# A graph and expert network of two layers: four late weight fills at slot 0, five result buffers, and the last sums on both sides of a branch

## The chip, the cores and the metric

The kernel runs on one core of a Trainium2 chip. The time is that of one execution on the device, in microseconds (us); of several runs the median is given. A profile of one more execution lies beside the times. Engines are called as in its rows: PE (TensorE; PEld is its weight load), DVE (VectorE), ACT (ScalarE), POOL (GpSimd), SP (SyncE); a "q" behind the name (SPq, ACTq) is the engine's issuing of transfers and its control instructions.

## What is computed

There are 2708 nodes with 256 features in float32 and a random adjacency matrix with some 1.2% of ones. Two layers follow one another; each is an attention over the graph and then a network of 8 experts, of which every node takes its best two. The part that the change touches is the expert network of the second layer:

```python
def moe(x):                       # 2708 x 256, E = 8, hidden 512
    gate = softmax(x @ gate_w + gate_b)
    w, e = top_k(gate, 2)         # two experts for each node
    out = 0
    for k in range(2):
        h = gelu(x @ W1[e[k]] + b1[e[k]])
        out += w[k] * (h @ W2[e[k]] + b2[e[k]])
    return x + out
```

The kernel computes each expert only for the nodes that chose it.

## The kernel before

**Rows and slots.** Each node's row, with its weight and its number, is scattered to a region of DRAM called `disp`, twice, into the region of each of its two experts. The expert network then works on chunks of 128 rows, one chunk in one "slot". Layer 1 always runs 47 slots (`often`, L1145). The first 20 are laid out before all rows are routed; the others are placed once routing is done (`place_grid`). Should an input need more than 47, a branch (`tc.If(used > often)`, L1986) runs the others. With this input it isn't taken.

**One slot.** `slot(s, s1)` (L1903) does this in the order of the program: it starts late weight fills, if any are due; `up` (L1830) makes the scaled bias `bias2` on ACT (L1837), 16 matmuls for the hidden layer (L1844) and four GELUs on ACT (L1852); `turned(s + 1)` transposes the next slot's rows on DVE (L1817); a step of the routing of the tiles still missing follows (`line.step()`, on DVE, POOL and PE); then `down(s - 1)` (L1858) runs eight matmuls of the slot before (L1860), fetches for slots to come, adds bias and weight to the result `y` on DVE (L1866), and POOL scatters `y` to its rows in `xd` (L1872). `xd1` has two rows for each node, one for each of its experts, so nothing is added there.

**What a slot fetches.** `fetch` (inside `slot`) gets weights three slots ahead by an indirect transfer of POOL (L1750), and the rows of a chunk six slots ahead (L1757, five in layer 0): SP reads the chunk's place from a table (L1762), then issues four transfers of a quarter each into a buffer `xg` (L1769) and one for the weights and numbers into `who` (L1775). `xg` is read by the transpose, `who` by the bias, by `y` and, as addresses, by the scatter; so a buffer of `who` comes free only when the scatter has landed. `y` too is held until its scatter has landed.

**Weights of layer 1.** Eight buffers (`ring`), one for each expert at first. Four are filled ahead; four lie in memory that the attention gives back late and are filled from within the slots by `fill(e)` (L1895), on ACT's queue, 1154 KB each.

**What sets the order.** In layer 1's slots PE, ACT and DVE keep the order of the program (a schedule written by hand, L1800), and SP does so in the whole kernel. Transfers issued by SP and ACT report on eight semaphores, taken in turn in one common order (101 to 108 in the trace); an issue waits until the transfer before it on the same semaphore has landed. POOL's transfers have eight of their own (110 to 117).

**The sums.** The result is `kept` (what came out of the attention) plus both rows of `xd1`. It is formed in parts (L2037ff): `whole_` are four parts of 512 nodes, which early slots have written in full; `rest` are the others (256, 256, 128 and 20 nodes). At the end of slot 40 (`s0`, L2089) SP loads the two rows of each part of `whole_` (8 loads of 512 KB, L2058), behind scatters 0 to 38. Three of the parts are added (L2069, L2070) and stored (L2073) after slots 43 to 45. After the last slot, `ending()` loads all but one part of `rest` on ACT's queue, adds and stores the last part of `whole_`, and loads the last part of `rest`, whose buffer that one had. Then comes the branch, and behind it the adds and stores of `rest` (L2130).

Of the kernel before, what the change touches and what calls it, by code (L numbers as in the profile page):

```python
# [9 lines left out]
F32 = mybir.dt.float32  # L10
# [10 lines left out]
P = 128  # L21
N = 2708
D = 256
# [11 lines left out]
GROUP = 4  # L35
# [64 lines left out]
ROWS_AHEAD = 5  # L100
# [6 lines left out]
def adj_ffn_kernel(ctx: ExitStack, tc: tile.TileContext, a: dict, out: bass.AP):  # L107
    nc = tc.nc
# [3 lines left out]
    rows = ctx.enter_context(tc.tile_pool(name="rows", bufs=3))  # L112
# [242 lines left out]
    class Line:  # L355
# [6 lines left out]
        def add(self, steps):  # L362
            self.waiting.append(steps)
# [765 lines left out]
    class Experts:  # L1129
# [293 lines left out]
                tc.declare_no_dep(start.ins, group=self.groups[2], reason="other rows of xd")  # L1423
                tc.add_to_no_dep_group(self.groups[3], start.ins)

        def behind_results(self, start, but=0):
            self.behind(start, self.results[: len(self.results) - but])

        def behind_written(self, start, last=True):
            self.behind(start, self.written)  # L1430
# [326 lines left out]
        def fetch_rows(self, s):  # L1757

            disp, wide = self.disp, D // GROUP
            xg = self.one.tile([P, GROUP, wide], F32, name="xg", bufs=self.rows_ahead + 2)  # L1760
            who = self.one.tile([P, 2], F32, name="who", bufs=self.rows_ahead + 3)
            at = nc.values_load(  # L1762
                self.token_row[0:1, s : s + 1], min_val=0, max_val=IDLE,
                engines=(mybir.EngineType.SP,),
                skip_runtime_bounds_check_because="a chunk begins below its region's end",
            )
            chunk = disp[bass.ds(at, P), :]
            starts = [
                nc.sync.dma_start(  # L1769
                    xg[g * QUARTER : (g + 1) * QUARTER],  # L1770
                    chunk[:, g * wide : (g + 1) * wide].rearrange("(t i) e -> i t e", t=GROUP),
                )
                for g in range(GROUP)
            ]
            starts.append(nc.sync.dma_start(who, chunk[:, D:]))  # L1775
            for i, start in enumerate(starts):
                if s < FULL_AFTER[self.early]:
                    self.other_rows(start, late=False)
                if s in (0, FULL_AFTER[self.early]):
                    self.behind_written(start, last=(i == GROUP))  # L1780
            return xg, who
# [25 lines left out]
        def slots(self, two, ps_mm, ps_acc, line):  # L1807
            hidden, own_norm, xd = self.hidden, self.own_norm, self.xd
            often = self.often
            _, hc, w2, b2, b1, ln, row = self.packed_weights  # L1810
# [19 lines left out]
            def up(w, xe, factor):  # L1830


                bias2 = two.tile([P, D], F32, name="bias2", bufs=2 if own_norm else 4)
                if own_norm:
                    nc.vector.tensor_scalar(bias2, w[:, b2:b1], factor, None, ALU.mult)
                else:
                    nc.scalar.activation(bias2, w[:, b2:b1], AF.Copy, scale=factor)  # L1837
                hT = two.tile([P, hc, P], F32, name="hT")
                for g in range(0, hc, GROUP):
                    ps = ps_mm.tile([P, GROUP, P], F32, name="mm")  # L1840
                    for i in range(GROUP):
                        f = g + i
                        for c in range(DC):
                            nc.tensor.matmul(  # L1844
                                ps[:, i, :],
                                w[:, c * hidden + f * P : c * hidden + (f + 1) * P],
                                xe[:, c, :],
                                start=(c == 0), stop=(c == DC - 1),
                            )
                    for i in range(GROUP):  # L1850
                        f = g + i
                        nc.scalar.activation(  # L1852
                            hT[:, f, :], ps[:, i, :], AF.Gelu, bias=w[:, b1 + f : b1 + f + 1]
                        )
                return hT, bias2

            def down(s, w, who, hT, bias2, then):
                ps = ps_acc.tile([P, D], F32, name="acc")  # L1858
                for f in range(hc):
                    nc.tensor.matmul(  # L1860
                        ps, hT[:, f, :], w[:, w2 + f * D : w2 + (f + 1) * D],
                        start=(f == 0), stop=(f == hc - 1),
                    )
                then()
                y = two.tile([P, D], F32, name="y", bufs=3)
                nc.vector.scalar_tensor_tensor(  # L1866
                    y, ps, who[:, 1:2], bias2, op0=ALU.mult, op1=ALU.add
                )
                at = bass.IndirectOffsetOnAxis(ap=who.bitcast(I32)[:, 0:1], axis=0)
                if not own_norm:  # L1870

                    start = nc.gpsimd.indirect_dma_start(  # L1872
                        xd[:], at, y, None, bounds_check=2 * N - 1, oob_is_err=False
                    )
                    for i in (2, 5):
                        tc.declare_no_dep(
                            start.ins, group=self.groups[i], reason="other rows of xd"
                        )
                    tc.add_to_no_dep_group(self.groups[2], start.ins)
                    self.results.append(start.ins)  # L1880
                    return
                start = nc.gpsimd.indirect_dma_start(  # L1882
                    xd[:], at, y, None, bounds_check=N - 1, oob_is_err=False, compute_op=ALU.add
                )
                if s < FULL_AFTER[self.early]:
                    tc.declare_no_dep(start.ins, group=self.groups[3], reason="other rows of xd")
                    tc.add_to_no_dep_group(self.groups[2], start.ins)
                self.last_start = start
                return start

            n = FULL_AFTER[self.early]
# [8 lines left out]
            fills = [] if own_norm else list(range(RING, E))  # L1900
            placed, placing, behind, xe = False, None, None, None

            def slot(s, s1):  # L1903
                nonlocal placed, placing, behind, xe
                w, (_, who) = self.weights[s], self.rows_[s]
                for _ in range((2, 0, 1, 1)[s] if s < 4 and fills else 0):
                    fill(fills.pop(0))
                after = turned(1) if s == 0 and not own_norm else None
                hT, bias2 = up(w, xe, who[:, 1:2])
# [57 lines left out]
            with tc.issue_after(self.last_start.ins) if own_norm else ExitStack():  # L1967
                i = 0 if own_norm else 1
# [36 lines left out]
    experts1 = Experts(1, 512, packed1, gb_b, False, xd1, disps[1], 14)  # L2005
# [7 lines left out]
    with tc.tile_pool(name="mask", bufs=1) as mp, ExitStack() as first_masks:  # L2013
# [16 lines left out]
        with tc.tile_pool(name="sum", bufs=1, side="right") as pool:  # L2030
            own = [pool.tile([P, GROUP, D], F32, name=f"y{i}") for i in range(GROUP)]
# [7 lines left out]
            whole_ = [x for x in parts_ if x[0] < DONE_EARLY]  # L2039
            rest = [x for x in parts_ if x[0] >= DONE_EARLY + GROUP]  # L2040
            rest = [(DONE_EARLY, 2, P), (DONE_EARLY + 2, 2, P), *rest]
            places = {x[0]: i % GROUP for i, x in enumerate(whole_ + rest)}

            def rows_of(dst, j, t, n, r):
                if n == 1:
# [3 lines left out]
                return rows_[:, t % GROUP : t % GROUP + n]  # L2049

            def results(t, n, r):
                i = places[t]
                return own[i][:r, :n], free[i][:r, :n]

            def load(parts_, queues, early=0):
                for i, (t, n, r) in enumerate(parts_):
                    for j, queue in enumerate(queues):
                        start = queue.dma_start(results(t, n, r)[j], rows_of(xd1, j, t, n, r))  # L2058
                        if early:
                            tc.declare_no_dep(  # L2060
                                start.ins, group=experts1.groups[2], reason="rows written"
                            )
                            tc.add_to_no_dep_group(experts1.groups[5], start.ins)
                        if i == 0:
                            experts1.behind_results(start, but=int(early))

            def add(t, n, r):
                y, y1 = results(t, n, r)
# [3 lines left out]
            def store(t, n, r):  # L2072
                nc.sync.dma_start(rows_of(out, 0, t, n, r), results(t, n, r)[0])  # L2073

            def again():
                load(whole_, (nc.sync, nc.sync))
                for x in whole_:
                    add(*x)
                    store(*x)
                load(rest, (nc.sync, nc.sync))  # L2080

            def ending():
                load(rest[:-1], (nc.scalar, nc.scalar))
                add(*whole_[-1])
                store(*whole_[-1])
                load(rest[-1:], (nc.scalar, nc.scalar))

            experts1.again, experts1.ending = again, ending
            s0 = experts1.sum_behind + 2  # L2089
            experts1.then = {s0: [partial(load, whole_, (nc.sync, nc.sync), 1)]}  # L2090
            for i, x in enumerate(whole_[:-1]):
                experts1.then[s0 + 3 + i] = [partial(add, *x), partial(store, *x)]
            experts1.run(line)
            for x in rest:
                add(*x)
                store(*x)


# [35 lines left out]
```

## Time and profile before

| | |
|---|---|
| runs of the kernel | 1190.30, 1190.56, 1183.24 us, median 1190.3 |
| the profiled execution | 1172.41 us, span of its instructions 1170.7 us |
| mean granted TensorE clock | 0.992 |
| layer 1's slots | from 974 us to 1152 us of the span |
| PE busy in the stretches of the prediction (974 to 1010, to 1045, to 1135) | 31.9 of 36, 32.6 of 35, 89.0 of 90 us |
| from the end of the last matmul to the end of the span | 18.7 us |

The span runs from the first to the last instruction of the core, and all starts in the views are counted from its beginning. A timeline row has start, length, engine, line, operation, what it writes from what it reads, and how many in a row; in brackets stands how long the engine was idle before and what ended the idle time. Rows of SPq and ACTq are the issuing of transfers, and a long one has waited in it. A row of waits has the total, the number and the longest. "mT" as a target of a load is memory of the masks, used again for the second rows of the sums.

### The profile page before, as it was taken

The numbers are of one execution on the slowest core, as the hardware profiler recorded it, in microseconds if no ns is written. First come the engines' busy times: TensorE is split into PE (matmuls) and PEld (weight loads), VectorE is DVE, ScalarE is ACT, GpSimd is POOL, SyncE is SP. The second block draws the span as 40 slices with busy tenths as digits, with TensorE's granted clock in tenths as the row PEclk, the third lists the DMA queues.
The fourth block names the chain that finished last, engine by engine and source line by source line (L and its number), as shares of the span: only waits on it lengthen the run. The fifth ranks groups of instructions, "written<-read, shape, count | busy, mean of one in ns | idle before, by whom it ended". The sixth has DMA issues, their size and how long they took to land. (4 is left out here: it accounts for less than half of the span.)

```text
span 1170.7 us, 20856 instructions
## 1 busy us (share of the span) xinstructions
PE 1122.7 (96%) x6421; PEld 910.6 (78%) x6421; DVE 648.6 (55%) x2406; ACT 415.4 (35%) x1232; POOL 427.7 (37%) x519
## 2 busy tenths in 40 slices
PE   8989999999999999999999999998999998999993
PEld 5665666666666666689999999997899997988993
DVE  5565777786886877653222222222876778632225
ACT  3222222212222222443333333332676664344441
POOL 3001212121222122453344343332663656866552
PEclk9999999999999999999999999999999999999997
DMA  9678676867754668569665945552100617577346
GB/s 220 135 161 212 172 185 159 241 162 183 219 136 141 154 149 313 160 187 279 186 193 130 334 116 162 139 169 59 56 1 29 214 50 212 146 246 240 79 115 248
DMA packets 198661, 195.88 MB, mean 167 GB/s; under 512 B 90939, under 2 KB 181524, under 8 KB 192520
## 3 DMA queue, kind: packets, MB, share of 16 engines
q1 hardware_dynamic: 172780, 117.51, 40.0%
q0 software_dynamic: 24256, 70.81, 19.0%
q10 hardware_dynamic: 1500, 6.08, 1.5%
q8 instruction: 55, 0.90, 0.3%
q14 instruction: 70, 0.57, 0.2%
HBM read 246.19 MB, written 66.15 MB: 267 GB/s over the span
## 5 line engine op out<-in xcount | busy, mean ns | idle before, releaser
L1844 PEld LDWEIGHTS mm<-xe,ring 128*128 128x128 f32 x2192 | 259.3, 193 | 16.9 <-DVE xe L1817 7.8
L1844 PE MATMUL mm<-xe,ring 128*128 128x128 f32 x2192 | 262.2, 277 | 7.7 <-DVE xe L1817 5.1
L1852 ACT ACTIVATE hT<-mm,ring 128x128 f32<-128x128 f32 x548 | 156.6, 369 | 286.4 <-issue 151.0
L1860 PE MATMUL acc<-ring,hT 128*128 128x256 f32 x1096 | 252.2, 380 | 0.0
L1860 PEld LDWEIGHTS acc<-ring,hT 128*128 128x128 f32 x1096 | 201.3, 190 | 24.9 <-ACT hT L1852 1.2
L650 PEld LDWEIGHTS acc<-v,p 128*128 128x128 f32 (+1 forms) x880 | 160.0, 190 | 62.4 <-issue 37.2
L650 PE MATMUL acc<-v,p 128*128 128x257 f32 (+1 forms) x880 | 202.7, 383 | 0.0
L586 PE MATMUL s<-g,xnT 128*128 128x512 f32 x420 | 200.3, 597 | 0.6 <-DVE mT L605 0.6
L1866 DVE SCALAR_TENSOR_TENSOR y<-acc,who,bias 128x256 f32<-128x256 f32 x92 | 44.4, 482 | 260.4 <-PE acc L1860 236.8
L1560 POOL DMA_INDIRECT disp<-row,to x88 | 91.3, 1038 | 257.4 <-DVE x L670 125.4
L598 ACT ACTIVATE p<-s 128x512 f32<-128x512 f32 x105 | 62.7, 597 | 194.6 <-PE s L586 178.4
L288 POOL TENSOR_TENSOR ln_rs<-ln_rs,minus_half 128x2 f32<-128x2 f32 x88 | 68.4, 778 | 172.5 <-DVE ln_rs L284 120.0
L930 PE MATMUL acc<-parts,m 128*128 128x266 f32 x924 | 126.3, 293 | 0.0
L930 PEld LDWEIGHTS acc<-parts,m 128*128 128x128 f32 x924 | 117.1, 185 | 4.1 <-ACT raw L957 0.9
L586 PEld LDWEIGHTS s<-g,xnT 128*128 128x128 f32 x420 | 76.8, 190 | 55.1 <-issue 50.3
L1750 POOL DMA_INDIRECT ring<-L_ffn_packed,weight_row x76 | 79.9, 1051 | 98.1 <-PE acc L1860 65.6
L601 DVE SCALAR_TENSOR_TENSOR p<-p,mT 128x512 f32<-128x512 f32 x100 | 71.0, 710 | 75.1 <-ACT p L598 74.9
L1882 POOL DMA_INDIRECT xd<-y,who x45 | 70.5, 1568 | 105.8 <-DVE xe L1823 53.6
L897 ACT CAST m<-mT 128x512 fp32r<-128x512 fp8e4 (+4 forms) x168 | 71.8, 475 | 9.7 <-PE acc L930 6.3
L1872 POOL DMA_INDIRECT xd<-y,who x47 | 49.6, 1056 | 44.9 <-DVE y L1866 40.0
L272 DVE SCALAR_TENSOR_TENSOR row<-x,wr_rows 128x256 f32<-128x256 f32 x128 | 54.4, 425 | 3.3
L1823 DVE TENSOR_SCALAR xe<-xe_raw,ring 128x128 f32<-128x128 f32 x90 | 27.2, 351 | 39.7 <-DMA ring<-L_ffn_packed,weight_row 38.7
(337 smaller groups left out, 1073.6 us busy)
## 6 DMA issues: line engine op xcount, KB each, us to landing
adj<-in_adj_dram SPq DMA_DIRECT2D x100, 256.0 KB
L_ffn_packed<-in_L_ffn_W_dram SPq DMA_DIRECT2D x32, 512.0 KB
xg<-disp SPq DMA_DIRECT2D x368, 32.0 KB
L_ffn_packed<-in_L_ffn_W_dram SPq DMA_DIRECT2D x32, 256.0 KB
neighbours<-mT SPq DMA_DIRECT2D x5, 1408.0 KB
mT<-neighbours SPq DMA_DIRECT2D x5, 1408.0 KB
ring<-L_ffn_packed SPq DMA_DIRECT2D x3, 2182.0 KB
xin<-in_x_dram SPq DMA_DIRECT2D x42, 128.0 KB
```

The source lines that it names most:

```text
L288: nc.gpsimd.tensor_tensor(rs[:r, 1], rs[:r, 0], minus_half[:r], ALU.pow)
L586: nc.tensor.matmul(ps[:kr, :nb], xnT[:, c, k0 : k0 + kr], g[:, c, :nb], start=(c == 0), stop=(c == DC - 1 and k < KEYS),)
L601: nc.vector.scalar_tensor_tensor(p, p, LARGEST, mask, op0=ALU.min, op1=ALU.mult)
L650: nc.tensor.matmul(accs[j][:r], p[keys, q0 : q0 + r], v[keys, k, :], start=(k == 0), stop=(k == NT - 1),)
L897: nc.scalar.copy(m[:, : q1 - q0], MASKS[b].of_key(mTs[b], k)[:, q0 - b * BN : q1 - b * BN],)
L930: nc.tensor.matmul(acc[:r], masks[t], parts[:, k, i], start=(k == 0 and i == 0), stop=False,)
L1560: nc.gpsimd.indirect_dma_start(disp[:], bass.IndirectOffsetOnAxis(ap=to[:r, j : j + 1], axis=0), rows2[:r, j], None,)
L1750: nc.gpsimd.indirect_dma_start(w, None, packed[:], bass.IndirectOffsetOnAxis(ap=self.weight_row[:, s : s + 1], axis=0), bounds_check=E * P ...
L1844: nc.tensor.matmul(ps[:, i, :], w[:, c * hidden + f * P : c * hidden + (f + 1) * P], xe[:, c, :], start=(c == 0), stop=(c == DC - 1),)
L1852: nc.scalar.activation(hT[:, f, :], ps[:, i, :], AF.Gelu, bias=w[:, b1 + f : b1 + f + 1])
L1860: nc.tensor.matmul(ps, hT[:, f, :], w[:, w2 + f * D : w2 + (f + 1) * D], start=(f == 0), stop=(f == hc - 1),)
L1882: start = nc.gpsimd.indirect_dma_start(xd[:], at, y, None, bounds_check=N - 1, oob_is_err=False, compute_op=ALU.add)
```

## The change

Six things are changed:

1. All four late fills start at slot 0 (before: two at slot 0, one each at slots 2 and 3).
2. `y` has five buffers in layer 1 (before 3), `bias2` three (before 4).
3. `xg` has `ROWS_AHEAD + 2` buffers, that is 7 in both layers (before 8 in layer 1), and `who` three more than before (12 in layer 1, 11 in layer 0).
4. The loads of the early sums are issued at the end of slot 39 (before: 40). The set of scatters that they wait for stays 0 to 38, but the exemption of the loads from scatters (`declare_no_dep`) is gone.
5. `ending()` loads all of `rest` with one row of each pair on SP's queue and the other on ACT's, and adds and stores the last part of `whole_` and all of `rest` ahead of the branch. Behind the branch nothing is left. In the branch, `again()` does all sums anew.
6. For that the parts of `rest` lie in buffers 0 (both halves), 1 and 2, which the parts stored early had.

```diff
-        def behind_results(self, start, but=0):
-            self.behind(start, self.results[: len(self.results) - but])
+        def behind_results(self, start):
+            self.behind(start, self.results)
...
-            xg = self.one.tile([P, GROUP, wide], F32, name="xg", bufs=self.rows_ahead + 2)
-            who = self.one.tile([P, 2], F32, name="who", bufs=self.rows_ahead + 3)
+            xg = self.one.tile([P, GROUP, wide], F32, name="xg", bufs=ROWS_AHEAD + 2)
+            who = self.one.tile([P, 2], F32, name="who", bufs=self.rows_ahead + 6)
...
-                bias2 = two.tile([P, D], F32, name="bias2", bufs=2 if own_norm else 4)
+                bias2 = two.tile([P, D], F32, name="bias2", bufs=2 if own_norm else 3)
...
-                y = two.tile([P, D], F32, name="y", bufs=3)
+                y = two.tile([P, D], F32, name="y", bufs=3 if own_norm else 5)
...
-                for _ in range((2, 0, 1, 1)[s] if s < 4 and fills else 0):
+                while fills:
                     fill(fills.pop(0))
...
-            places = {x[0]: i % GROUP for i, x in enumerate(whole_ + rest)}
+            places = {x[0]: (i, 0) for i, x in enumerate(whole_)}
+            places.update({x[0]: p for x, p in zip(rest, ((0, 0), (0, 2), (1, 0), (2, 0)))})
...
                         if early:
-                            tc.declare_no_dep(
-                                start.ins, group=experts1.groups[2], reason="rows written"
-                            )
                             tc.add_to_no_dep_group(experts1.groups[5], start.ins)
                         if i == 0:
-                            experts1.behind_results(start, but=int(early))
+                            experts1.behind_results(start)
...
                 load(rest, (nc.sync, nc.sync))
+                for x in rest:
+                    add(*x)
+                    store(*x)
 
             def ending():
-                load(rest[:-1], (nc.scalar, nc.scalar))
-                add(*whole_[-1])
-                store(*whole_[-1])
-                load(rest[-1:], (nc.scalar, nc.scalar))
+                load(rest, (nc.sync, nc.scalar))
+                for x in (whole_[-1], *rest):
+                    add(*x)
+                    store(*x)
...
-            experts1.then = {s0: [partial(load, whole_, (nc.sync, nc.sync), 1)]}
+            experts1.then = {s0 - 1: [partial(load, whole_, (nc.sync, nc.sync), 1)]}
...
             experts1.run(line)
-            for x in rest:
-                add(*x)
-                store(*x)
```

More of the change, by code (lines that the diff above doesn't have):

```diff
@@ L2051, in results @@
             def results(t, n, r):
-                i = places[t]
-                return own[i][:r, :n], free[i][:r, :n]
+                i, j = places[t]
+                return own[i][:r, j : j + n], free[i][:r, j : j + n]
             def load(parts_, queues, early=0):
```

## The prediction

> **What bounds the kernel now.** I read the busy table and its slices first, then busy time by stage, the waits of layer 1's expert network, and the timelines around each edit.
>
> ```profile
> PE 1122.7 (96%) x6421; PEld 910.6 (78%) x6421; DVE 648.6 (55%) x2406; ACT 415.4 (35%) x1232; POOL 427.7 (37%) x519
> ```
>
> TensorE is busy 96% of the span, so only its gaps are to be won. By stage (columns: stretch, length, then busy us of PE, PEld, DVE, ACT, POOL, the granted clock, DMA share, GB/s):
>
> ```profile
> 974.00:1010.00 36.00, 31.88 (x215) 28.11 (x215) 25.90 (x130) 14.43 (x44) 27.45 (x31) 1.00 0.71 217
> 1010.00:1045.00 35.00, 32.59 (x223) 30.02 (x222) 16.40 (x64) 13.85 (x45) 26.75 (x28) 1.00 0.66 184
> 1045.00:1135.00 90.00, 89.01 (x607) 83.36 (x607) 22.22 (x52) 39.41 (x127) 51.64 (x51) 1.00 0.54 153
> ```
>
> Those are the 47 slots of layer 1, which start up() every 3.51 us where nothing waits. By the starts of up(), slots 2 to 8 lose 6.0 us (routing on POOL and DVE is their bound), slot 14 loses 2.6, slot 17 0.5, slot 26 1.4: 10.6 in all. After 1152.0 no matmul runs and 18.7 us of ending follow. The change touches three places: slot 0, slots 14 and 17, and slot 40 with the ending.
>
> **The four fills.** Before, two late weight buffers (1154 KB each) are filled at slot 0, the others at slots 2 and 3. The SyncE and ScalarE timelines:
>
> ```profile
> 974.34 5.95 SPq L1769 DMA_DIRECT2D xg<-disp  x4
> 982.02 2.93 SPq L1769 DMA_DIRECT2D xg<-disp  x4
> ```
> ```profile
> 974.13 0.83 ACTq L1896 DMA_DIRECT2D ring<-L_ffn_packed  x2
> 985.20 0.33 ACTq L1896 DMA_DIRECT2D ring<-L_ffn_packed  x1
> 985.63 0.51 ACT L1837 ACTIVATE bias<-ring,who 128x256 f32<-128x256 f32 x1 [3.61 <-DMA xg<-disp]
> 991.44 0.37 ACTq L1896 DMA_DIRECT2D ring<-L_ffn_packed  x1
> 991.86 0.51 ACT L1837 ACTIVATE bias<-ring,who 128x256 f32<-128x256 f32 x1 [4.69 <-DMA xg<-disp]
> ```
>
> The trace's transfers, each with its semaphore and its landing, show the rule here: an issue of SP or ACT first waits until the previous transfer on its semaphore has landed; eight semaphores go round in one order for both queues. So fill 3 waited for a piece of row 3 (landed 985.18) and held ScalarE, as fill 4 did. Before that cost little, because routing was later still. At slot 0 the same waits stand ahead of bias(0), gelu(0) and thus of down(0).
>
> Fills 1 and 2 took semaphores six places apart. If I go on at that spacing, fill 3 takes that of row 3's first piece (landed 980.77, behind fill 1), and fill 4 that of row 4's first piece, which lands behind fill 3. Fills land 4.31 apart (979.95, 984.26), so fill 3 lands at 988.6 and row 4's piece at about 989. ScalarE issues fill 4 then, loads its table (1.28 at 978.14 before), and gelu(0) starts at about 991.2 instead of 979.44; down(0) follows at 991.6 (was 979.86, +11.7), its y at 993.5 (was 984.62, +8.9). VectorE keeps program order, so routing steps and turns behind that y move with it: +8.9. Some 1 us of the later ScalarE holds is given back.
>
> Here a rule speaks against the change. The longest gap inside these slots is 2.24 us and the granted clock stays 1.00, so no row shows TensorE after a long idle. The Trainium skill, "TensorE: Matmul & The Clock Gate", part 1 ("What's actually happening"), says an idle window of about 3.4 us halves the clock until it has been busy as long again. After 11.7 us idle that is an estimated 1.7 us; by the row it is 0. I take the rule: **fills +9.6**.
>
> A second rule speaks for the change: "DMA: Bandwidth & Descriptors", "Queues, rings and completion order", says each DMA engine takes turns between queue rows packet by packet. Then rows of SP would slip between the fills and cost some 0. The trace says otherwise: row 3's second piece, issued 974.84, landed 984.61, just behind fill 2 (984.26), where pieces elsewhere take 1.4 to 1.9. The measurement decides. Bounds: if ScalarE isn't held, row 3 lands behind all four fills at about 993, its turn moves from 986.34 by 7, less 1: +6. Below: 0, if rows slip through; a gain only up to the 6 that these slots lose, which the routing chain excludes. Above: +12, with fill 4 behind one more fill.
>
> **Five y buffers.** y(s) waits until scatter(s-3) has landed; POOL issues these late, behind routing, pads and weights. VectorE's waits and slot 14:
>
> ```profile
> DVE y L1866 <- DMA xd<-y,who: 18.9, 7, 5.4
> ```
> ```profile
> 1031.40 0.48 DVE L1866 SCALAR_TENSOR_TENSOR y<-acc,who,bias 128x256 f32<-128x256 f32 x1 [4.30 <-DMA xd<-y,who]
> 1031.80 0.43 DVE L1817 STREAM_TRANSPOSE xe<-xg 128x256 f32<-128x256 f32 x1
> ...
> 1032.29 1.94 PE L1844 MATMUL mm<-xe,ring 128*128 128x128 f32 x15 [2.24 <-DVE xe L1817]
> ```
>
> y(11) waits 4.30, the turn of slot 14 stands behind it, and TensorE idles 2.24. With five, y(11) needs scatter(6), issued 1014.71, where its sum is ready at 1026.6; y(14) needs scatter(9), issued 1031.49, with its sum ready at 1039.6. Slots 14 and 17 get back 2.6 + 0.5: **-3.1** (0 if weights become what is late next; -3.1 is the whole loss).
>
> **bias2 3, xg 7, who 12.** bias(s) needs y(s-3) done: in steady slots that ends 1.9 us before, so 0; without y's gain it would have cost up to 2. The new xg wait is for turn(k-7): row 46 was issued at 1133.39, turn(39) at 1119.01. 0. SP loses its 2.58 us wait for scatter 8 ahead of who(17); TensorE doesn't see it. Layer 0's SP waits (108 us) also shrink, under a TensorE that is 98.8 to 100% busy there: 0. Slot 26's 1.4 came from a row landing behind a weight fetch; it may go or double: 0, +-1.4.
>
> **Loads of early sums at slot 39.** They wait for the same scatters 0 to 38 as now. Each load waits by itself now, at 0.03 us for a semaphore instruction on SP: under 1 us in all, with row 46's fetch the only thing queued behind it.
>
> ```profile
> 1133.39 1.84 SPq L1769 DMA_DIRECT2D xg<-disp  x4
> 1135.96 0.37 SPq L2058 DMA_DIRECT2D y<-xd  x1
> ...
> 1139.50 0.46 SPq L2058 DMA_DIRECT2D mT<-xd  x1
> ...
> 1145.99 0.44 DVE L1817 STREAM_TRANSPOSE xe<-xg 128x256 f32<-128x256 f32 x1
> ```
>
> The eight loads took 13.84 us from 1135.96 to the last landing. Scatter 38 landed at 1130.14; with slots 6.5 later (9.6 - 3.1) that is 1136.6, the last load lands at 1150.5, row 46 half a us behind it, and its turn is due at 1152.5: **0**. If the slots are early instead (fills 0, y -3.1), loads start at 1130.4, row 46 lands at 1144.8 against a turn at 1142.9: +1.9. Upper end +4.7.
>
> **The ending.** Now the rest's eight loads go on ACT alone, 1155.75 to 1161.47, and the sums come after the branch: VectorE stands 7.86 us for SP, whose own branch is the second view (columns: duration, then first and last start).
>
> ```profile
> 1163.94 1.47 DVE L2069 TENSOR_TENSOR y<-y,kept 128x512 f32<-128x512 f32 x2 [7.86 <-SPq L1986]
> ```
> ```profile
> L1986 SPq COMPARE_BRANCH  x1: 50/50/50, 1156.5 to 1156.5; - x1
> L1986 SPq EVENT_SEMAPHORE  x9: 17/17/17, 1162.2 to 1164.8; - x9
> ```
>
> After: on two queues the loads are issued by 1157.6, the sums (4.2 us of VectorE, 1163.94 to 1167.95) run from 1159.3 to some 1164.5, the last store is issued at 1164.9. But SP reaches its branch only then, and its branch took 5.7 us before its next instruction (PE's 3.96, POOL's 2.84, ACT's 2.5). With 2.5 to 3.7 and 2.5 us of closing waits: 1170.3 to 1171.5 against 1170.7. **0**, from -2 (a short branch) to +3 (the full 5.7 and late loads). What the branch holds anew isn't run here: 47 slots are enough.
>
> **Sum:** 9.6 - 3.1 + 0 + 0 = +6.5: span 1177.2, profiled execution 1172.41 + 6.5 = 1178.9. The runs' median is 17.9 above that execution; adding the same 6.5 gives **1196.8**, +0.5%.
>
> **Rivals.** (A, likeliest, 0.40) as summed. (B, 0.20) ScalarE isn't held, only row 3 is late: +6 - 3.1 = +2.9, 1193.2. For it: the wait depends on semaphores dealt out anew. Against: fills 3 and 4 both waited. (C, 0.15, not slower) Row pieces pass the fills: 0 - 3.1 + 1.9 = -1.2, 1189.1, and with a short branch 1187. Decides: row 3 landing before 986. Against: 984.61. (D, 0.20, clearly slower) Fill 4's semaphore belongs to a transfer behind one more fill: another 4.3 at slot 0, and down(0) past 996; +10.8, and with the full branch +3 at the end 1204. It decides once gelu(0) starts after 995. (E, 0.05) The adds before the branch save their 4.2 and the loads' 2 us, and slots 2 to 8 gain as well: 1182, at the best 1178: the gaps of slots 14 and 17, slot 26, 2 of slots 2 to 8, 3 to 6 of the ending. That the change doesn't do as it says is in B: two fills wait where they did.
>
> **Numbers.** About 1% (11.9) can be told from no change. Slower by over 1%: D, 0.20, and of A the three in ten in which its own upper costs (row 46, the full branch) come together, 0.12: 0.32. Faster by over 1%: 0.03 of E. Within: the rest, 0.65. Range 1184 to 1211: C with its short branch less 3, D with row 46's 4.7 and the slot 26 loss; A alone 1190 to 1204.
>
> **What would show it.** Right: gelu(0) near 991, a TensorE gap of over 10 us at slot 0, no y wait at slot 14, row 46 no wait, stores before the branch, an end some 18.7 after the last matmul. Wrong: row 3 landing by 986, down(0) before 985, or an SP branch that costs under 1 us.

## The result, and the profile after

In the first comparison the changed kernel took 1195.2 us in the median (1191.1 to 1204.6), the kernel before 1188.8 on the same chips: ratio 1.0062, 95% interval [1.0037, 1.0087], which is +7.4 us; the medians differ by 6.4. (Below, a ratio with two numbers in brackets is always this: time over that of before, and its interval.) It was compared twice more: 1.0093 [1.0056, 1.0130] and 1.0084 [1.0053, 1.0115]. The forecast was +6.5, 1.0055.

One thing has to be known ahead of all profiles. The profiled execution of before, 1172.4 us, isn't like the runs of these comparisons. The runs were made on several chips: on some, before takes 1189 us and stands still for some 12 us at slots 10 to 13 (below: the stall), on one it takes 1178 and doesn't. Each of those chips served for one set of runs, so a difference of chips can't be told from one of occasions. The profile shown ahead of the prediction has no stall, that of the changed kernel has it. So their 23.4 us of difference in span are not what the change cost; the numbers below are taken against profiles or runs of the same kind, unless another is named.

The page of the changed kernel, and its busy time by stage (columns as above):

```profile
span 1194.1 us, 20924 instructions
PE 1131.7 (95%) x6421; PEld 917.9 (77%) x6421; DVE 648.3 (54%) x2406; ACT 413.9 (35%) x1232; POOL 429.4 (36%) x519
```
```profile
974.00:1010.00 36.00, 23.68 (x152) 20.14 (x150) 20.55 (x105) 10.95 (x35) 17.52 (x21) 0.86 0.64 199
1010.00:1045.00 35.00, 26.81 (x159) 23.98 (x159) 15.32 (x74) 10.03 (x33) 26.10 (x28) 0.85 0.42 104
1045.00:1135.00 90.00, 88.76 (x605) 83.37 (x604) 26.49 (x80) 38.21 (x125) 50.05 (x49) 1.00 0.60 179
```

The second profile of before, on a chip of the same kind, has these stages:

```profile
974.00:1010.00 36.00, 32.15 (x220) 27.73 (x220) 26.97 (x140) 14.81 (x47) 26.08 (x31) 1.00 0.72 216
1010.00:1045.00 35.00, 26.27 (x153) 22.82 (x152) 14.72 (x60) 9.22 (x30) 22.71 (x23) 0.85 0.39 98
```

Slots start at 980.3 in it and at 980.8 in the changed kernel (the start of a slot is here and below the first weight load of its up()), so the stages can be compared: PE loses 8.5 us in the first (32.15 to 23.68) and nothing in the second (26.27 and 26.81; both have the stall, of 12.7 and 12.5 us). So the change's loss lies at slots 0 to 5. The ScalarE timeline of the changed kernel shows the hold, and TensorE's its price:

```profile
978.95 14.58 ACTq L1896 DMA_DIRECT2D ring<-L_ffn_packed  x4
993.57 0.51 ACT L1837 ACTIVATE bias<-ring,who 128x256 f32<-128x256 f32 x1 [14.31 <-DMA xg<-disp]
994.10 1.28 ACT L1852 ACT_TABLE_LOAD   x1
995.39 1.14 ACT L1852 ACTIVATE hT<-mm,ring 128x128 f32<-128x128 f32 x4
```
```profile
980.87 3.81 PE L1844 MATMUL mm<-xe,ring 128*128 128x128 f32 x32
995.81 3.78 PE L1860 MATMUL acc<-ring,hT 128*128 128x256 f32 x8 [11.13 <-ACT hT L1852]
...
999.49 2.35 PE L1844 MATMUL mm<-xe,ring 128*128 128x128 f32 x16
1001.68 1.89 PE L1860 MATMUL acc<-ring,hT 128*128 128x256 f32 x8
```

The four issues hold ScalarE for 14.58 us. gelu(0) starts 16.4 us behind the first fill (forecast 991.2 - 974.1 = 17.1), and TensorE idles 11.13 (forecast 11.7). The first eight matmuls after it take 3.78 where 1.89 is their time, and the granted clock of the stage falls from 1.00 to 0.86: 1.9 us by the row, and some 0.3 more in the sixteen behind them (2.35 instead of some 2.0). The prediction's estimate from the Trainium skill ("TensorE: Matmul & The Clock Gate", part 1) was 1.7.

### The profile page after: what moved, and what is told of

It reads as the page before. It is cut to its first block, busy times and chain, and to the rows that moved or that the text cites. A ratio compares the mean times of both kernels' runs of the same rounds, so it can differ in the third digit from the quotient of the medians.

```text
span 1194.1 us, 20924 instructions
## 1 busy us (share of the span) xinstructions
PE 1131.7 (95%) x6421; PEld 917.9 (77%) x6421; DVE 648.3 (54%) x2406; ACT 413.9 (35%) x1232; POOL 429.4 (36%) x519
## 5 line engine op out<-in xcount | busy, mean ns | idle before, releaser
L1844 PE MATMUL mm<-xe,ring 128*128 128x128 f32 x2192 | 264.6, 278 | 11.5 <-DVE xe L1817 8.4
L1860 PE MATMUL acc<-ring,hT 128*128 128x256 f32 x1096 | 255.2, 383 | 11.1 <-ACT hT L1852 11.1
```

The costliest lines, as they stand in the source:

```text
L1844: nc.tensor.matmul(ps[:, i, :], w[:, c * hidden + f * P : c * hidden + (f + 1) * P], xe[:, c, :], start=(c == 0), stop=(c == DC - 1),)
L1860: nc.tensor.matmul(ps, hT[:, f, :], w[:, w2 + f * D : w2 + (f + 1) * D], start=(f == 0), stop=(f == hc - 1),)
```

## The experiments

up() of slot 5 minus up() of slot 0 is called the head below; slots 10 to 13 at 3.51 each would take 14.0 us, and what they take more is the stall's loss. "Before" without a number is the run beside it on the same chip.

**1. Both kernels once more.** No edit.

> The kernel before, profiled once more. The two profiled executions differ by 23.4 us, the medians only by 6.4. If the profile shown of before was an ordinary one, this span is 1168 to 1174 again and up() of slots 9 to 13 goes on at 3.51 us. If stalls like those at slots 10, 11 and 13 of the changed kernel's profile (12.5 us) belong to both kernels, the span is 1180 to 1195 and shows some of them somewhere.

Measured: 1.0010 [0.9994, 1.0025], span 1186.8. Head 21.1 us, slots 10 to 13 take 26.8, a loss of 12.7. The stall in VectorE's timeline and SyncE's:

```profile
1013.04 0.43 DVE L1817 STREAM_TRANSPOSE xe<-xg 128x256 f32<-128x256 f32 x1
1020.05 0.17 DVE L1231 COPY n_late<-misc 128x8 f32<-128x8 f32 x1 [6.58 <-PE acc L1860]
...
1027.22 0.48 DVE L1866 SCALAR_TENSOR_TENSOR y<-acc,who,bias 128x256 f32<-128x256 f32 x1 [6.74 <-remote]
1027.62 0.43 DVE L1817 STREAM_TRANSPOSE xe<-xg 128x256 f32<-128x256 f32 x1
```
```profile
1018.56 0.01 SPq L1775 DMA_DIRECT2D who<-disp  x1
1020.71 4.31 SPq L1769 DMA_DIRECT2D xg<-disp  x4
1026.45 0.70 SPq L1775 DMA_DIRECT2D who<-disp  x1
```
```profile
1014.72 0.17 PE L1228 MATMUL misc<-counted,ones 128*128 128x8 bf16 x1
...
1020.75 0.38 PE L1860 MATMUL acc<-ring,hT 128*128 128x256 f32 x1 [0.35 <-issue]
```

VectorE stands still twice, for 6.58 and 6.74 us. The first time it goes on 5.2 us after the end of the matmul whose `misc` it reads (L1228), the second time 6.1 us after the last matmul into `acc`. SyncE's instructions, mostly 0.35 us or less each elsewhere, come one or a few in every 0.70 us. The stall is in all nine profiles on such chips, of before, of the changed kernel and of those between them, and so none of the change's doing.

> The changed kernel once more. My theory: slots 0 to 4 cost about 10 us more than before in any profile (gelu(0) some 16.5 us behind the first fill, TensorE idle 12 to 13 us between up(1) and down(0)). The rival, that the stalls of slots 10 to 13 come from the change, has these at the same place again, 10 us or more; mine has them elsewhere, smaller or not at all. Time 1.005 to 1.009 of before.

Measured: 1.0093 [1.0056, 1.0130], just above the time expected. The head is 28.7, so only +7.6, for ScalarE is held for less this time, 11.94 us, and TensorE idles 8.51, not 12 to 13:

```profile
982.27 11.94 ACTq L1896 DMA_DIRECT2D ring<-L_ffn_packed  x4
996.08 1.14 ACT L1852 ACTIVATE hT<-mm,ring 128x128 f32<-128x128 f32 x4
```
```profile
996.50 3.78 PE L1860 MATMUL acc<-ring,hT 128*128 128x256 f32 x8 [8.51 <-ACT hT L1852]
```

Slots 10 to 13 lose 15.7, three us more than before's 12.7. The stall is thus at the same place, as the rival said, but it is before's too. The same kernel a third time, with the other runs of experiment 4:

> The changed kernel on another chip. Before took 1189 on the chips of the first two comparisons and 1178 on that of the third, where its stall at slots 10 to 13 is missing. If the fills' cost is the change's own, slots 2 to 4 lose 10 us more than before here too (TensorE idle between up(1) and down(0)), and what follows depends on the chip: with no stall, the waits of slots 14, 17, 20 and 26 (some 4 us) vanish under the delay, so +5 to +7 us, 1.004 to 1.007. If the cost were the stall's, 1.000 here on a chip without it.

Measured: 1.0084 [1.0053, 1.0115], beside a before of 1189.3, again with the stall, so the part of the expectation about another kind of chip stays untried. Head 28.5 (+7.4, where 10 was expected), with ScalarE held for 11.81 us and TensorE idle for 8.38; stall 12.6.

**2. The fills apart.** Before, with

```diff
-                for _ in range((2, 0, 1, 1)[s] if s < 4 and fills else 0):
+                while fills:
```

> Before with one edit: all four fills at slot 0. Theory (fills +9.6, net of the rest -3.1): 1.008 of before, some 9 to 11 us more, down(0) 15 us behind up(0) as in the changed kernel. Rival (the loss is at slots 10 to 13, from the buffers): 1.000 to 1.003.

Measured: 1.0050 [1.0033, 1.0066]; head 29.1, stall 15.1. Again, beside the changed kernel:

> Before with all four fills at slot 0, beside the changed kernel on the same chip. Theory: the fills make all of the loss, and their delay hides the other edits: within 0.3% of the changed kernel, 1.004 to 1.008. Rival: the buffers or the order of the loads carry half of it: 1.002 or less here.

Measured: 1.0056 [1.0035, 1.0077]; head 31.4. Both are some 6 us, with intervals from 4 to 9. In the head they lose 8.0 and 10.3 more than before; of the 2.8 us that before loses at slots 27 and 45 they lose 1.0 and 0.2. The fills do cost; 9 to 11 was too much for the whole kernel. Up(46) minus up(0) is 8.8 and 10.1 longer than in the second profile of before; the medians say less, and single profiles don't settle 3 us (up(0) itself starts anywhere from 976.0 to 984.2 in them).

Now the changed kernel without them, the same lines the other way:

> The changed kernel with the fills at slots 0, 2 and 3 as before, all else changed. Theory: -3.1 of the y buffers and 0 of the rest, 0.997 of before; no y wait at slots 11 and 14. Rival: 1.004 or more, since the other edits cost.

Measured: 1.0103 [1.0063, 1.0142]. The theory of 0.997 falls: what is left of the change costs as much as all of it (1.0093 in the same set of runs). Repeated:

> The changed kernel with the old fills, once more. It was at 1.010 on a chip with the stall, where SyncE was 3 to 5 us ahead of the turns and row 46 came late. On a chip without it, theory: the loads ahead of row 46 still cost 1 to 4 us at slots 45 and 46 and y's gain is given back at slots 20 and 21 (rows behind weights): 1.000 to 1.004. With the stall: 1.007 to 1.013 again.

Measured: 1.0081 [1.0058, 1.0104], on a chip with the stall, as that case had it. Its head is 21.1 and its stall 12.5, as before's; the changed kernel beside it is at 1.0084. Against the second profile of before it loses 3.1 more at slot 18, 2.9 at slots 24 to 28 and 3.8 at slots 45 and 46, together 9.8, and 0.4 less elsewhere: up(46) minus up(0) grew by 9.4 (190.9 and 181.5). The turns wait for rows. Slot 46, on SyncE, VectorE and TensorE:

```profile
1158.57 0.39 SPq L2059 DMA_DIRECT2D y<-xd  x1
...
1162.14 0.48 SPq L2059 DMA_DIRECT2D mT<-xd  x1
1163.38 3.20 SPq L1769 DMA_DIRECT2D xg<-disp  x4
1173.21 0.45 DVE L1817 STREAM_TRANSPOSE xe<-xg 128x256 f32<-128x256 f32 x1 [5.22 <-DMA xg<-disp]
1173.71 2.67 PE L1844 MATMUL mm<-xe,ring 128*128 128x128 f32 x14 [4.64 <-DVE xe L1817]
```

Row 46 is issued at 1163.4 behind eight loads and turned ten us later; up(46) starts 8.4 behind up(45).

**3. The other parts, on a chip without the stall** (before 1178.0). The buffers: before, with

```diff
-            xg = ... bufs=self.rows_ahead + 2)
+            xg = ... bufs=ROWS_AHEAD + 2)
-                bias2 = ... bufs=2 if own_norm else 4)
+                bias2 = ... bufs=2 if own_norm else 3)
-                y = ... bufs=3)
+                y = ... bufs=3 if own_norm else 5)
```

> Before with the buffers of y, bias2 and xg of the changed kernel (5, 3, 7), all else as it was. My prediction: 0.997 of before (-3.1 us). The rival, from the second profile of before, in which y never waits for its scatter at slots 11 and 14: 0.999 to 1.002, since there is no such wait in an ordinary execution.

Measured: 0.9999 [0.9981, 1.0018]. The waits of y for its scatter are gone and slots 14 and 17 run at 3.51, as forecast. But the rival's reason is wrong here too, for with three buffers the wait is there on this chip: there is no profile of before itself on it, but those of the next two kernels, which leave `y` alone, lose 2.6 and 2.8 us at slot 14. The one with the loads moved, in VectorE's timeline:

```profile
1037.85 0.48 DVE L1866 SCALAR_TENSOR_TENSOR y<-acc,who,bias 128x256 f32<-128x256 f32 x1 [3.62 <-DMA xd<-y,who]
```

What is won there is lost further on with five buffers. VectorE and SyncE at slots 20 and 21:

```profile
1053.65 0.45 DVE L1817 STREAM_TRANSPOSE xe<-xg 128x256 f32<-128x256 f32 x1 [5.45 <-DMA xg<-disp]
```
```profile
1043.23 7.74 SPq L1769 DMA_DIRECT2D xg<-disp  x4
```

Slot 20 now starts 6.85 behind slot 19, slot 21 5.06 behind that: 4.9 us lost. Row 20 was issued by 1041.7 and turned at 1053.65. In that stretch POOL issues a weight fetch of 1154 KB every 2.65 us, catching up (1036.83, 1039.49, 1042.15, 1044.80, 1047.44), and rows land among them: the four pieces of row 20 at 1050.6 to 1053.6, the three fetches issued from 1039.49 to 1044.80 at 1048.8, 1052.4 and 1053.0. In the first profile of before, whose slots begin at the same time (976.0 and 976.1), it landed no later, at 1053.0. up(20) stood at 1053.7 there and stands at 1054.2 with five buffers: TensorE got there sooner and waited.

The loads: before, with

```diff
-            experts1.then = {s0: [partial(load, whole_, (nc.sync, nc.sync), 1)]}
+            experts1.then = {s0 - 1: [partial(load, whole_, (nc.sync, nc.sync), 1)]}
```

and, as in the change, no `but` and no exemption from the scatters.

> Before with one edit: the loads of the early sums at the end of slot 39, ahead of row 46's fetch on SyncE. My prediction's lower end: 0 to +1.9. The rival, after the changed kernel with its old fills lost 7 us at slots 45 and 46: SyncE is only 5 us ahead of the turns here, so row 46 is late: up(46) 3 us or more behind its 3.51, and 1.003 to 1.007 of before.

Measured: 1.0012 [0.9990, 1.0033]: no difference that the time shows. In its profile up(46) comes 6.24 behind up(45), 2.7 more than before, so the mechanism is there and its size between the two expectations.

The ending: before, with the new `places`, `results`, `again` and `ending()`, and nothing behind the branch.

> Before with one edit: the new ending (rest loaded on two queues, all sums ahead of the branch). My prediction: 0 (-2 to +3 us). From the profiles with it: 18.2 us from the last y to the end against 18.7, so -0.5: 0.999 to 1.000 of before.

Measured: 0.9983 [0.9970, 0.9995], median 1175.9 against 1178.0. It is the only version whose interval lies below before, by 2 us (0.6 to 3.5). Its profile doesn't say where: from the start of the last y to the end it has 19.0 us, the first profile of before 18.7.

> The changed kernel with the old fills and with the loads of the early sums behind row 46's fetch again (they wait for scatters 0 to 39 here). If the order on SyncE makes the loss of the kernel with old fills alone (1.010), this one is at 1.000 to 1.004 and slots 45 and 46 lose under 3 us; if it is something else (the buffers, the ending), it stays at 1.007 or more.

(Edit: that of the old fills, and `s0` for `s0 - 1`.) Measured: 1.0007 [0.9991, 1.0024]. It is within the first case, and slots 45 and 46 lose 2.1; but since this chip has no stall, and the kernel with the loads at slot 39 wasn't run on it, the order of the loads isn't shown by this pair alone to be what made 1.010.

**4. Do the fills cover the loads?** The changed kernel with `s0` for `s0 - 1`:

> The changed kernel with the early sums' loads behind row 46's fetch (waiting for scatters 0 to 39). Theory: under the fills' delay SyncE is far enough ahead, row 46 is not late either way, so the order of the loads is worth 0 to 1 us here: within 0.2% of the changed kernel. Rival: it wins back 4 us or more, as without the fills.

Measured: 1.0063 [1.0039, 1.0086], beside 1.0084 for the changed kernel on the same chip; the intervals overlap, and the medians are the same (1197.2). Slot 46 runs at 3.51 instead of 5.72 there (4.07 and 3.52 in the other two profiles of the changed kernel). So under the fills the order of the loads is worth 0 to 2 us, and without them slots 45 and 46 lost 5.7 to 7.2 us, where before lost 2.0 on such a chip. SyncE's lead, the time from its issuing a row's last piece to that row's turn, goes with it. At row 43 it is 3.5 and 5.0 us in the two runs of the kernel with old fills, and slot 46 loses 4.6 and 4.9; in the changed kernel it is 9.5, 12.4 and 15.3, and slot 46 loses 2.2, 0.6 and 0. The lead is longer by a delay of TensorE that SyncE doesn't share.

## Why the prediction came out, step by step

**Fills, +9.6: the mechanism was right, the size too large.** ScalarE is held at slot 0 by the semaphores, TensorE stands until gelu(0), and starts with a cold clock (1.9 us). But the transfers that hold it were guessed wrong. Fill 3 waited for row 2's `who`, not for row 3's first piece; fill 4 for row 3's fourth piece, which had the semaphore of fill 1 in between, not for a piece of row 4. In the profile shown, that piece was issued at 984.9, once fill 1 had landed, and landed at 993.2, right behind fill 3 at 993.0. So the outcome there, fill 4 behind fill 3, is the forecast one by luck. In the other two profiles of the changed kernel, fill 3 itself was held until 8.2 and 9.5 us behind fill 1; the piece landed right behind fill 2, and fill 4 was issued before fill 3 had landed. Hence two sizes: ScalarE held for 14.6, or for 11.9 and 11.8; the head 10.2, or 7.6 and 7.4 us longer than before's. The three profiles of other kernels with four fills at slot 0 show the same two (held 14.7, 14.5 and 12.4). In the whole time the fills alone cost 6. Of the 8.0 and 10.3 that the head lost there, slots 27 and 45 give back 1.8 and 2.6; single profiles don't settle more.

Rival B (ScalarE not held) is out by the holds; D needed gelu(0) 21 us behind the first fill (13.7 to 16.4 in the three). C (rows slip between fills) is out because row 3's pieces landed right behind the fill ahead of them each time, so that the packet rule that the prediction took from the Trainium skill ("DMA: Bandwidth & Descriptors", "Queues, rings and completion order") made no difference here either. But C's sign, row 3 landing by 986, 11.9 us behind the first fill, did come in two of the three profiles (11.6 and 11.5), with no row past a fill: it could not tell C from A.

**Five y buffers, -3.1: wrong.** This is the step that failed outright. Slots 14 and 17 gave up their waits, as said; what I set aside as "0 if weights become what is late next" is what happened, at slot 20. The whole edit measured 0.9999. On the chips with the stall there was nothing to win, as far as one profile tells: the second of before has slots 14 and 17 at 3.40 and 3.51. I read one execution as typical, while the runs shown beside it, 11 to 18 us longer, said that it wasn't.

**Row 46, 0 under the fills: nearly right**, 0 to 2.2. Its reason held (slots later than SyncE); without the fills slot 46 loses 4.6 and 4.9, as much as the upper end of 4.7, and slot 45 more.

**bias2, xg, who, slot 26: 0** under the fills, for slots 14 to 44 of the changed kernel run at 3.51 but for 0.2 us at slot 41. Without the fills, on chips with the stall, slots 18 and 24 to 28 lose 4 to 6 us more than before, on late rows, so 0 was wrong there. Which buffer does that, I didn't separate, but the profiles without four fills at slot 0 point to `who`: slots 24 to 28 lose 2.6 to 3.6 us in the three with twelve buffers of it (with and without the stall) and 0 to 1.3 in the five with nine, of which one has the change's `y`, `bias2` and `xg` and loses 0.0.

**The ending, 0: right within its range.** Its parts went as told. SyncE's stores and its branch in the changed kernel:

```profile
1183.18 4.33 SPq L2071 DMA_DIRECT2D out_dram<-y  x5
```
```profile
L1986 SPq COMPARE_BRANCH  x1: 50/50/50, 1187.6 to 1187.6; - x1
L1986 SPq EVENT_SEMAPHORE  x9: 17/17/17, 1190.2 to 1190.8; - x9
```

The last store is issued ahead of the branch, and the branch takes 2.6 us, of the 2.5 to 3.7 assumed. From the start of the last y to the end it is 18.2 to 19.9 us in the eight profiles with the new ending and 18.4 to 19.4 in the six with the old, so this stretch shows no gain. Alone, the ending won 2.0 in the time, the lower end.

**The sum, +6.5: near, and partly by luck.** The three ratios are 7.4, 10.0 and 11.1 us. Alone, the fills cost some 3 less than forecast and the y buffers won 3.1 less: two misses that cancel. And the terms don't add as I added them: on chips with the stall the fills alone cost 6 us, all the rest alone 10 to 12, both together 7 to 11; in the same set of runs the fills add nothing that shows to the rest (1.0084 and 1.0081, 1.0093 and 1.0103). The delay that the fills make is also the lead that SyncE needs, and it covers what the other edits make late. The profiles show that for slots 18, 24 to 28 and 46; that it is the whole of it isn't shown. What the changed kernel takes on a chip without the stall wasn't measured.

**Open:** what the stall is, and why some chips have it; where the ending's 2 us lie; whether `who` alone makes rows late at slots 18 and 24 to 28.

## What to carry to other kernels

When a transfer moves ahead on a compute engine's queue, look up what its issue will wait for, not only what it moves: here four issues of 0.3 to 0.4 us held ScalarE for 12 to 15. A wait removed in a stretch where a queue is catching up is only moved to where the queue sets the pace; compare the start of the first slot behind the stretch, not the wait. And put the profiled execution beside the runs before costing waits of a few us from it.

## What the runs showed of the hardware that was not expected

On some chips an execution of either kernel has stretches, mostly from 1000 us on, in which SyncE gets through one or a few instructions every 0.70 us, and in the one shown VectorE goes on 5 to 6 us after the matmuls that it waited for: 12.5 to 15.7 us are lost at slots 10 to 13. On the other chip no such stall is in any of four profiles. And the branch at L1986, which this input passes by, took SyncE 3.9 to 5.7 us to its next instruction in the six profiles with the old ending and 2.6 to 2.8 in the eight with the new one, in which the loads and sums come ahead of it. Why, no run here shows.
